# Turning softmax weights between attention and its values: 32x32 blocks on VectorE and DMA in the place of 128x128 turns on TensorE

## The chip, the cores and the metric

The kernel runs on one core of a Trainium2 chip, in one launch. The metric is device microseconds of that core, from runs without the profiler. A profiled execution of the kernel before gives the views below; times inside it are microseconds from the start of its span.

## The reference

Inputs are `x` (2 batches, 1024 tokens, 256 features), a context of 77 rows per batch, and the weights. Four residual layers follow one another, each on a layer normalization of `x` (no scale, no shift), all in 32-bit floats:

```python
x = x + cross_attention(ln(x), ctx, mask)            # 16 heads of 16, 77 keys
x = x + routed_attention(ln(x))                      # 4 of 16 heads of 64 per batch, 1024 keys
x = x + gelu(ln(x) @ ctx.T) @ ctx                    # 77 hidden units
x = x + moe(ln(x))                                   # 8 experts, one per token, 256 -> 1024 -> 256
```

The change lies in the second layer. Per batch, four heads are chosen by the mean over tokens of a router's logits. For each chosen head:

```python
score = softmax(Q @ K.T / 8)      # 1024 queries x 1024 keys
O = score @ V                     # then the 4 heads side by side, @ Wo + bo
```

The product with V sums over keys, and TensorE sums over partitions. The scores come out with queries on the partitions, so their exponentials have to be turned until keys lie on the partitions.

## The kernel before, in words

**Stages.** The kernel has three stages, with an order of instructions that is written out by hand for TensorE, VectorE, ScalarE and GpSimd (`tc.manual_schedule`). Stage "a" is cross attention, one step per tile of 128 tokens. Stage "b" is routed attention, with the third layer, the layer norms and the routing of the fourth worked in between. The tail and the expert blocks come last: 20 blocks of 128 token slots, each with its own expert weights of 2 MB.

**Items of stage b.** An item `i` is one tile of 128 queries with two heads (`m` names which two of the four); there are 32 (`NI`). Two tiles `q` = 0, 1 of the same two heads are a pair, `gm` (`TG` = 2). `split(i)` gives `gm, g, m, q`. Step `s` of stage b (`b_step`, L778) works on several items at once, in this order on each engine:

- `b_scores` (L693): for each of the two heads a PSUM tile `bsc` of 128 queries x 1024 keys, four matmuls in all. The pool `big` holds two such tiles, so the next item's scores need this item's exponentials to be done with them.
- `b_weights` (L712): VectorE finds the negative maximum of each row (L716); ScalarE takes the exponentials into `be` in SBUF and sums each row (L718).
- `b_transposed` (L722), called four times for the item of the step before: TensorE turns four 128x128 blocks of `be` into a PSUM tile `bpt` (L728), and ScalarE or VectorE copies it to `beT` (L729), two of the four each.
- `b_values` (L731), for the item three steps back (`VA`): half of the keys of a whole pair, 256 queries wide, into the PSUM tile `bov` that stays open for two steps (L738).
- `b_inverse_sums` (L744): VectorE inverts the sums, GpSimd spreads them over 64 columns; `b_turned_sums` (L752): TensorE turns these, ScalarE copies them to `brT`; `b_normalized` (L761): VectorE multiplies `bov` by `brT` into `boT` (L763), once per pair.
- `b_projected` (L765): from `boT` the output projection, added to `xs` (L774), five steps after the item's scores (`PR`).

**What fills the steps.** `at("b", s, pos, f, ...)` puts a piece of other work into step `s` at position 0, 2 or 3, and `take` runs it there: the projections of the routed heads (`b_qk` L646, `b_v` L665), the third layer (`do_rows "c"`, `do_turn "c"`, `c_hidden`, `gelu`, `c_out`), the routing of the fourth (`do_rows "d"`, `d_logits`, `d_expert`), and at the end of the stage the first expert list (`first_blocks`, `first_slots`, `first_tokens`, L1349 to L1367). `route_heads` (L570) of batch 1 runs in step 3 and has SP load that batch's chosen weights, 16 DMAs. Stage b's SBUF pool is `ebp` (L1470) with two buffers per tag.

**Queues.** DMAs of `ln_rows` (rows for the experts to DRAM, L305 and L306), of the routed weights (L612, L623) and of the expert weights (`block_loads`, L1083) are issued by SP, whose order the scheduler chose before. Rows of the expert blocks are gathered and scattered by GpSimd.

Of the kernel before, what the change touches and what calls it, by code (L numbers as in the profile page):

```python
# [20 lines left out]
P = 128  # L21
# [18 lines left out]
def kernel(  # L40
# [253 lines left out]
    def ln_rows(tag, t0, mv, rs, eng, y_out=None):  # L294

        ys = []
        for i in range(2):
            y = ynp.tile([P, D], F32, name=f"y_{tag}_{t0 + i}", tag="y")
            eng.tensor_scalar(
                y, xs[:, t0 + i, :], mv[:, i, 0:1], rs[:, i : i + 1], ALU.subtract, ALU.mult  # L300
            )
            ys.append(y)
            if y_out is not None:
                r0 = (t0 + i) * P
                nc.sync.dma_start(y_out[r0 : r0 + P, :D], y)  # L305
                nc.sync.dma_start(y_out[r0 : r0 + P, D:], xs[:, t0 + i, :])  # L306
        return ys

# [219 lines left out]
    sel, qks, vs = {}, {}, {}  # L528
    NP = NA // 2
# [116 lines left out]
    def b_qk(b, k, m, n, pool=accp, ptag="acc"):  # L646

        w, bc, _ = sel[b]
        if (b, k, m) not in qks:
            qks[b, k, m] = qkp[b].tile([P, S], F32, name=f"{k}T_{b}_{m}", tag=f"{k}T{m}")  # L650
        ps = pool.tile([P, 512], F32, name=f"bps_{b}_{m}_{k}_{n}", tag=ptag)
        for c in range(C):
# [6 lines left out]
            )  # L659
        nc.scalar.activation(  # L660
            qks[b, k, m][:, n : n + 512], ps, AF.Identity, bias=bc[k][:, m : m + 1],
# [3 lines left out]
    def b_v(b, t, pool=trp, ptag="tr"):  # L665
# [12 lines left out]
        nc.vector.tensor_tensor(vs[b][:, t], ps, bv, ALU.add)  # L678

# [13 lines left out]
    def b_scores(i):  # L693
# [15 lines left out]
        bes[i] = ebp.tile([P, 2, S], F32, name=f"be_{i}", tag="be")  # L709
        return sc  # L710

    def b_weights(i, sc):  # L712
        gm, g, m, q = split(i)
        for h in range(2):
# [4 lines left out]
                bes[i][:, h], sc[h], AF.Exp, bias=nm, accum_out=sms[g][:, q, s : s + 1]  # L719
            )  # L720

    def b_transposed(i, h, k0, copy):  # L722
        gm, g, m, q = split(i)
        if q == 0 and h == 0 and k0 == 0:
            beTs[gm] = ebp.tile([P, 2, NT, TG * P], F32, name=f"beT_{gm}", tag="beT")
        pt = trp.tile([P, 4, P], F32, name=f"bpt_{i}_{h}_{k0}", tag="tr")
        for k in range(k0, k0 + 4):
            nc.tensor.transpose(pt[:, k - k0, :], bes[i][:, h, k * P : (k + 1) * P], ident)  # L728
        copy(beTs[gm][:, h, k0 : k0 + 4, q * P : (q + 1) * P], pt)  # L729

    def b_values(i):  # L731
        gm, g, m, q = split(i)
        if q == 0:
            ovs[gm] = accp.tile([P, TG * P], F32, name=f"bov_{gm}", tag="acc")
        per = NT // TG
        for k in range(q * per, (q + 1) * per):
            for h in range(2):
                nc.tensor.matmul(  # L738
                    ovs[gm][h * FD : (h + 1) * FD, :],
                    lhsT=vs[g * TG // NT][:, k, 2 * m + h, :], rhs=beTs[gm][:, h, k, :],  # L740
# [20 lines left out]
    def b_normalized(gm):  # L761
        oT = oTs[gm] = ap_.tile([P, TG * P], F32, name=f"boT_{gm}", tag="boT", bufs=4)
        nc.vector.tensor_tensor(oT, ovs.pop(gm), rTs.pop(gm), ALU.mult)  # L763
# [12 lines left out]
    VA, PR = TG + 1, 2 * TG + 1  # L776

    def b_step(s):  # L778
# [3 lines left out]
        sc = b_scores(i) if i < NI else None  # L782
        take("b", s, 0)
        if 0 <= k < NI and k % TG == TG - 1:
            b_turned_sums(k // TG)
        if 0 <= j < NI:
            b_transposed(j, 0, 0, nc.scalar.copy)
        if i < NI:
            b_weights(i, sc)
        if 0 <= j < NI:  # L790
            b_transposed(j, 0, 4, nc.vector.tensor_copy)
        take("b", s, 2)
        if 0 <= k < NI:
            b_values(k)
        if 0 <= j < NI:
            b_transposed(j, 1, 0, nc.vector.tensor_copy)
            b_transposed(j, 1, 4, nc.scalar.copy)
            del bes[j]
            if j % TG == TG - 1:
                b_inverse_sums(j // TG)  # L800
        if 0 <= k < NI and k % TG == TG - 1:
            b_normalized(k // TG)
# [8 lines left out]
    def c_hidden(t0):  # L811
        b = t0 // NT
        yT = yTs.pop(("c", t0))
        ps = accp.tile([KC, 2 * P], F32, name=f"gps_{t0}", tag="acc")
# [6 lines left out]
    def c_gelu(t0):  # L821
# [8 lines left out]
        nc.vector.scalar_tensor_tensor(g, g, 1.0, ps, ALU.add, ALU.mult)  # L830

# [391 lines left out]
    def do_y(tag, t0, eng=nc.vector):  # L1223
        rows[tag, t0] = ln_rows(tag, t0, *rows[tag, t0], eng, ztok if tag == "d" else None)

    def do_rows(tag, t0, bias=None):

        do_power(tag, t0)
        do_y(tag, t0, nc.gpsimd)
        if bias is not None:  # L1230
            add_bias(t0, 2, bias)

# [66 lines left out]
    for t in range(NT):  # L1299
        at(*(("a", 18, 3), ("a", 18, 3), ("b", 0, 3), ("b", 0, 3),  # L1300
             ("b", 1, 2), ("b", 1, 2), ("b", 2, 2), ("b", 2, 2))[t], b_v, 0, t, *(acc if t > 3 else tr))
    for s, pos, k, m, n, *pool in (
        (5, 2, "k", 0, 0), (5, 3, "k", 0, 512), (6, 2, "q", 0, 0), (6, 3, "k", 1, 0),
        (7, 2, "k", 1, 512), (8, 2, "q", 1, 0), (19, 0, "q", 0, 512, *tr), (21, 0, "q", 1, 512, *tr),
    ):
        at("b", s, pos, b_qk, 1, k, m, n, *pool)
    for t in range(NT):
        at("b", 8 + t, 0, b_v, 1, t)

    def gelu(t0):  # L1310
        every(c_gelu(t0))

    for g in range(T // TG):
        s, t0 = 4 * g, TG * g
        if s + 13 < NI:
            at("b", s + 8, 3, do_rows, "c", t0)
            at("b", s + 9, 3, do_turn, "c", t0, *acc)
            at("b", s + 10, 2, c_hidden, t0)
            at("b", s + 10, 3, gelu, t0)
            at("b", s + 11, 2, c_out, t0)  # L1320
            at("b", s + 11, 3, do_rows, "d", t0)
            at("b", s + 13, 0, do_turn, "d", t0)
# [4 lines left out]
    at("b", 28, 3, do_rows, "c", t0)  # L1327
    at("b", 29, 3, do_turn, "c", t0, *acc)
    at("b", 30, 2, c_hidden, t0)
    at("b", 30, 3, gelu, t0)  # L1330
# [212 lines left out]
```

## Time and profile before

| what | us |
|---|---|
| median of 3 runs (622.35 to 623.37) | 623.32 |
| the profiled execution's own time | 623.49 |
| its span | 621.8 |
| TensorE busy, of the span | 581.7 |
| VectorE busy | 359.9 |
| ScalarE busy | 234.7 |
| GpSimd busy | 162.0 |

In the profile, PE is TensorE's matmuls, PEld its weight loads, which overlap them, DVE is VectorE, ACT ScalarE, POOL GpSimd, SP the engine that only issues DMAs. A line such as `L728 PE MATMUL bpt<-ident,be` names the line of the kernel, the engine, the operation, and the tile that is written and those that are read; then follow the shape, how often it occurs (`x512`), busy time in all, mean nanoseconds of one, and how long the engine was idle just before these instructions and which instruction ended most of that wait. A matmul of 32-bit floats shows as two instructions; a turn as one. In a view of stretches each row begins with the stretch and its length, then has the busy time of each engine in it, the granted TensorE clock as a share, the share of the DMA engines' time that was used, and GB/s.

Stage a ends and stage b begins near 152; the last scores of stage b start at 404.75; the steady run of expert blocks begins near 489 and lasts to the end.

### The profile page before, as it was taken

To read this page: it belongs to the slowest core of one execution; us is meant where nothing else is said; L and a number is where in the kernel's file an instruction comes from. 1 tells how busy PE (TensorE), PEld (TensorE's weight loads), DVE (VectorE), ACT (ScalarE), POOL (GpSimd) and SP (SyncE) were. 2 spreads that over 40 slices of the span, in tenths; PEclk is the share of its full clock that TensorE was granted. 3 is DMA by queue.
4 is the path that set the end of the run, shared out by engine and by line. 5 is a ranking of instruction groups with operands and counts; after the bars stand their busy time and mean duration, and the time that the engine had idled before them with its cause. 6 is when DMAs were issued, how large, how long until landed. Compare 5 with 4: busy or idle time off the path is not lost. (4 is left out here: it accounts for less than half of the span.)

```text
span 621.8 us, 10102 instructions
## 1 busy us (share of the span) xinstructions
PE 581.7 (94%) x3722; PEld 429.3 (69%) x3722; DVE 359.9 (58%) x939; ACT 234.7 (38%) x476; POOL 162.0 (26%) x204
## 2 busy tenths in 40 slices
PE   5999999989999999999999999996797999999994
PEld 4578878866655556656555656564596999999994
DVE  6767667852874356658665767676546433333331
ACT  3555545542655355445445555440021012111110
POOL 6656233222200020403021222200401233333321
PEclk9999999999999999999999999997689899999998
DMA  7100000020001000001000100011993799999940
GB/s 233 34 2 2 1 0 2 1 61 1 1 19 41 1 1 18 17 1 36 1 34 1 35 2 34 2 35 72 353 338 119 255 362 323 360 372 371 344 144 11
DMA packets 49674, 62.75 MB, mean 101 GB/s; under 512 B 11513, under 2 KB 42708, under 8 KB 49622
## 3 DMA queue, kind: packets, MB, share of 16 engines
q1 hardware_dynamic: 46352, 54.04, 25.8%
q0 software_dynamic: 2560, 7.34, 3.2%
q8 instruction: 31, 0.51, 0.3%
q10 hardware_dynamic: 709, 0.68, 0.3%
q14 instruction: 22, 0.17, 0.1%
HBM read 55.76 MB, written 6.82 MB: 101 GB/s over the span
## 5 line engine op out<-in xcount | busy, mean ns | idle before, releaser
L716 DVE TENSOR_REDUCE bnm<-bsc 128x1 f32<-128x1024 f32 x64 | 75.2, 1216 | 14.9 <-PE bsc L702 14.9
L1131 PE MATMUL ph<-ybT,w1s 128*128 128x128 f32 x640 | 79.7, 284 | 3.9 <-DVE ybT L1116 3.9
L1131 PEld LDWEIGHTS ph<-ybT,w1s 128*128 128x128 f32 x640 | 78.4, 200 | 6.0 <-DVE ybT L1116 5.1
L728 PE MATMUL bpt<-ident,be 128*128 128x128 f32 x512 | 73.1, 280 | 3.2 <-DVE v L678 1.2
L1150 PE MATMUL epo<-w2s,ehT 128*128 128x256 f32 x320 | 75.6, 380 | 0.0
L728 PEld LDWEIGHTS bpt<-ident,be 128*128 128x128 f32 x512 | 55.6, 140 | 27.9 <-issue 10.1
L718 ACT ACTIVATE be<-bsc,bnm 128x1024 f32<-128x1024 f32 x64 | 70.8, 1113 | 8.3 <-DVE bnm L716 7.9
L729 DVE COPY beT<-bpt 128x512 f32<-128x512 f32 x64 | 43.9, 686 | 50.4 <-PE bpt L728 50.4
L1138 ACT ACTIVATE ehT<-ph,b1s 128x128 f32<-128x128 f32 x80 | 22.9, 369 | 116.3 <-PE ph L1131 115.1
L702 PE MATMUL bsc<-kT,qT 64*128 64x512 f32 x256 | 64.6, 615 | 0.0
L738 PE MATMUL bov<-beT,v 128*64 128x256 f32 x512 | 63.4, 391 | 0.0
L1150 PEld LDWEIGHTS epo<-w2s,ehT 128*128 128x128 f32 x320 | 57.9, 190 | 6.3
L729 ACT COPY beT<-bpt 128x512 f32<-128x512 f32 x64 | 37.5, 586 | 62.4 <-PE bpt L728 61.4
L1140 DVE TENSOR_SCALAR ehT<-ph,b1s 128x128 f32<-128x128 f32 x80 | 22.5, 343 | 61.2 <-ACT ehT L1138 56.8
L738 PEld LDWEIGHTS bov<-beT,v 128*64 128x64 f32 x512 | 34.4, 139 | 24.6 <-issue 9.4
L1162 POOL DMA_INDIRECT out_dram<-ob,etok x20 | 20.5, 1023 | 94.2 <-DMA out_dram<-ob,etok 40.5
L750 POOL COPY brb<-brc 128x256 f32<-128x256 f32 x16 | 6.4, 398 | 146.5 <-DVE brc L748 146.5
L702 PEld LDWEIGHTS bsc<-kT,qT 64*128 64x128 f32 x256 | 22.5, 186 | 25.1 <-issue 20.7
L477 PE MATMUL av<-vblk,eT 128*128 128x51 f32 x320 | 37.4, 272 | 0.8 <-DVE hn L485 0.8
L477 PEld LDWEIGHTS av<-vblk,eT 128*128 128x128 f32 x320 | 37.1, 192 | 1.6 <-DVE hn L485 1.1
L453 DVE TENSOR_REDUCE mx<-sc 128x8 f32<-128x616 f32 x32 | 25.3, 792 | 16.6 <-PE sc L439 16.6
L469 ACT COPY eT<-pt 128x512 f32<-128x512 f32 (+1 forms) x48 | 23.0, 515 | 25.9 <-PE pt L468 25.1
(253 smaller groups left out, 854.2 us busy)
## 6 DMA issues: line engine op xcount, KB each, us to landing
w1s<-in_L_ffn_w_dram SPq DMA_DIRECT2D x20, 1024.0 KB
w2s<-in_L_ffn_w_dram SPq DMA_DIRECT2D x20, 1024.0 KB
b2s<-in_L_ffn_b_dram SPq DMA_DIRECT2D x20, 128.0 KB
xs<-in_x_dram SPq DMA_DIRECT2D x4, 512.0 KB
ztok<-xs SPq DMA_DIRECT2D x16, 128.0 KB
ztok<-y_d SPq DMA_DIRECT2D x16, 128.0 KB
ws_k<-in_L_ffn_Wk_dram SPq DMA_DIRECT2D x8, 64.0 KB
ws_q<-in_L_ffn_Wq_dram SPq DMA_DIRECT2D x8, 64.0 KB
```

Of the source, the lines that this page charges most:

```text
L453: nc.vector.tensor_reduce(mx, scv, AX.X, ALU.max)
L469: copy(eTs[t][:, c0 : c0 + n, :], pt[:, :n, :])
L477: nc.tensor.matmul(av[:, h0 : h0 + HW, :].rearrange("p h d -> p (h d)"), lhsT=eT[:, c, :], rhs=vblk[:, t // NT, c].rearrange("p h d -> p ( ...
L702: nc.tensor.matmul(sc[h][:, n : n + 512], lhsT=qks[b, "q", m][r, q0 : q0 + P], rhs=qks[b, "k", m][r, n : n + 512], start=True, stop=True,)
L716: nc.vector.tensor_reduce(nm, sc[h], AX.X, ALU.max, negate=True)
L718: nc.scalar.activation(bes[i][:, h], sc[h], AF.Exp, bias=nm, accum_out=sms[g][:, q, s : s + 1])
L728: nc.tensor.transpose(pt[:, k - k0, :], bes[i][:, h, k * P : (k + 1) * P], ident)
L729: copy(beTs[gm][:, h, k0 : k0 + 4, q * P : (q + 1) * P], pt)
L738: nc.tensor.matmul(ovs[gm][h * FD : (h + 1) * FD, :], lhsT=vs[g * TG // NT][:, k, 2 * m + h, :], rhs=beTs[gm][:, h, k, :], start=(k == 0), ...
L1131: nc.tensor.matmul(ph[:, f, :], lhsT=ws[n][0][:, c, f * P : (f + 1) * P], rhs=ybT[:, c, :], start=(c == 0), stop=(c == C - 1),)
L1138: nc.scalar.activation(hT[:, f, :], ph[:, f, :], AF.Relu, bias=b1s[:, f : f + 1])
L1150: nc.tensor.matmul(po, lhsT=hT[:, f, :], rhs=w2s[:, f, :], start=(f == 0), stop=(f == FC - 1))
```

## The change

The turn of `be` is done in two halves. VectorE turns `be` in place, in blocks of 32x32 (`b_turned`); that leaves each block turned but on its old quarter of the partitions. SP then issues 16 DMAs per pair (`b_moved`), each of 32 partitions x 4 KB, from quarter `g` of `be` to quarter `k` of `beT`. To make each of these one contiguous run per partition, the keys are stored in another order (the k-half of `b_qk`, and the reshaped `be`). TensorE turns none of it.

Along with that:

- `be` is one tile per pair and not per item; the values of an item are summed in one step over all 1024 keys and 128 queries, read in runs of 32 columns, and normalized per item;
- `VA` goes from 3 to 4 and `PR` from 5 to 4; the stage has one step less;
- the turns of an item stand at the start of the next step, ahead of that step's reduces on VectorE; the reciprocal of the sums stands ahead of the second item's turns;
- SP's order is now that of the program text, too; storing the rows for the experts is its own function at its own place (`store_rows`);
- many pieces of other work move by a step or a position, those of the end of the stage a step earlier, and `gelu` is spread over three positions.

```diff
+    def store_rows(t0, y_out):
+
+        for i, y in enumerate(rows["d", t0]):
+            r0 = (t0 + i) * P
+            nc.sync.dma_start(y_out[r0 : r0 + P, :D], y)
+            nc.sync.dma_start(y_out[r0 : r0 + P, D:], xs[:, t0 + i, :])
...
+    QD, QL = 4, 32
...
+        if k == "k":
+            out = qks[b, k, m].rearrange("p (g t l) -> p t g l", g=QD, l=QL)[:, n // P : n // P + 4]
+            ps = ps.rearrange("p (t g l) -> p t g l", g=QD, l=QL)
         nc.scalar.activation(
-            qks[b, k, m][:, n : n + 512], ps, AF.Identity, bias=bc[k][:, m : m + 1],
+            out, ps, AF.Identity, bias=bc[k][:, m : m + 1],
...
-        bes[i] = ebp.tile([P, 2, S], F32, name=f"be_{i}", tag="be")
+        if q == 0:
+            bes[gm] = ebp.tile([P, QD, TG, 2, S // QD], F32, name=f"be_{gm}", tag="be")
...
-                bes[i][:, h], sc[h], AF.Exp, bias=nm, accum_out=sms[g][:, q, s : s + 1]
-            )
-
-    def b_transposed(i, h, k0, copy):
+                bes[gm][:, :, q, h, :], sc[h].rearrange("p (g x) -> p g x", g=QD), AF.Exp, bias=nm,
+                accum_out=sms[g][:, q, s : s + 1],
+            )
+
+    def b_turned(i):
+
         gm, g, m, q = split(i)
-        if q == 0 and h == 0 and k0 == 0:
-            beTs[gm] = ebp.tile([P, 2, NT, TG * P], F32, name=f"beT_{gm}", tag="beT")
-        pt = trp.tile([P, 4, P], F32, name=f"bpt_{i}_{h}_{k0}", tag="tr")
-        for k in range(k0, k0 + 4):
-            nc.tensor.transpose(pt[:, k - k0, :], bes[i][:, h, k * P : (k + 1) * P], ident)
-        copy(beTs[gm][:, h, k0 : k0 + 4, q * P : (q + 1) * P], pt)
+        for h in range(2):
+            e = bes[gm][:, :, q, h, :]
+            nc.vector.transpose(e, e)
+
+    def b_moved(gm):
+
+
+        e = bes.pop(gm)
+        eT = beTs[gm] = ebp.tile([P, QD, TG, 2, NT, QL], F32, name=f"beT_{gm}", tag="beT")
+        for k in range(QD):
+            for g in range(QD):
+                nc.sync.dma_start(
+                    eT[k * QL : (k + 1) * QL, g].rearrange("l q h t x -> l (q h t x)"),
+                    e[g * QL : (g + 1) * QL, k].rearrange("l q h x -> l (q h x)"),
+                )
 
     def b_values(i):
         gm, g, m, q = split(i)
-        if q == 0:
-            ovs[gm] = accp.tile([P, TG * P], F32, name=f"bov_{gm}", tag="acc")
-        per = NT // TG
-        for k in range(q * per, (q + 1) * per):
+        ov = ovs[i] = accp.tile([P, P], F32, name=f"bov_{i}", tag="acc")
+        eT = beTs[gm]
+        for k in range(NT):
             for h in range(2):
                 nc.tensor.matmul(
-                    ovs[gm][h * FD : (h + 1) * FD, :],
-                    lhsT=vs[g * TG // NT][:, k, 2 * m + h, :], rhs=beTs[gm][:, h, k, :],
+                    ov[h * FD : (h + 1) * FD, :].rearrange("p (g x) -> p g x", g=QD),
+                    lhsT=vs[g * TG // NT][:, k, 2 * m + h, :], rhs=eT[:, :, q, h, k, :],
                     start=(k == 0), stop=(k == NT - 1),
                 )
...
-    VA, PR = TG + 1, 2 * TG + 1
+    VA, PR = 4, 4
...
         sc = b_scores(i) if i < NI else None
+        if 0 <= j < NI:
+            if j % TG == TG - 1:
+                b_inverse_sums(j // TG)
+            b_turned(j)
+            if j % TG == TG - 1:
+                b_moved(j // TG)
         take("b", s, 0)
-        if 0 <= k < NI and k % TG == TG - 1:
-            b_turned_sums(k // TG)
-        if 0 <= j < NI:
-            b_transposed(j, 0, 0, nc.scalar.copy)
         if i < NI:
             b_weights(i, sc)
-        if 0 <= j < NI:
-            b_transposed(j, 0, 4, nc.vector.tensor_copy)
-        take("b", s, 2)
         if 0 <= k < NI:
             b_values(k)
-        if 0 <= j < NI:
-            b_transposed(j, 1, 0, nc.vector.tensor_copy)
-            b_transposed(j, 1, 4, nc.scalar.copy)
-            del bes[j]
-            if j % TG == TG - 1:
-                b_inverse_sums(j // TG)
-        if 0 <= k < NI and k % TG == TG - 1:
-            b_normalized(k // TG)
+            b_normalized(k)
+        if 0 <= j < NI and j % TG == TG - 1:
+            b_turned_sums(j // TG)
+        take("b", s, 2)
...
-    at("b", 31, 2, do_power, "d", t0)
-    at("b", 31, 3, do_y, "d", t0)
-    at("b", 32, 2, do_turn, "d", t0, *acc)
-    at("b", 32, 3, d_logits, t0)
+    at("b", 30, 3, do_power, "d", t0)
+    at("b", 31, 2, do_y, "d", t0)
+    at("b", 32, 0, do_turn, "d", t0)
+    at("b", 32, 2, d_logits, t0)
...
-    at("b", 32, 3, do_power, "c", t0)
+    at("b", 31, 3, do_power, "c", t0)
...
-    at("b", 33, 3, first_blocks)
-    at("b", 33, 3, do_turn, "c", T1, *acc)
-    at("b", 34, 0, first_slots)
-    at("b", 35, 0, first_tokens)
+    at("b", 32, 3, first_blocks)
+    at("b", 32, 3, do_turn, "c", T1)
+    at("b", 33, 2, first_slots)
...
-            mybir.EngineType.Pool,
+            mybir.EngineType.Pool, mybir.EngineType.SP,
...
-            if s == NI + VA:
+            if s == NI + VA - 1:
                 stage_b.close()
+                pools["h"] = ctx.enter_context(tc.tile_pool(name="hp", bufs=2, side="right"))
                 pools["w", 1] = ctx.enter_context(tc.tile_pool(name="w1p", bufs=2, side="right"))
+                first_tokens()
```

## The prediction

> **What bounds the kernel now.** I read the page's engine shares and costliest groups first, then the busy times of the stretch in which routed attention runs (first scores to end of step 31), then the same for a cycle of four steps, then the order of instructions in two steps and at the end of the stage. From the page:
>
> ```profile
> PE 581.7 (94%) x3722; PEld 429.3 (69%) x3722; DVE 359.9 (58%) x939; ACT 234.7 (38%) x476; POOL 162.0 (26%) x204
> ...
> L716 DVE TENSOR_REDUCE bnm<-bsc 128x1 f32<-128x1024 f32 x64 | 75.2, 1216 | 14.9 <-PE bsc L702 14.9
> ...
> L728 PE MATMUL bpt<-ident,be 128*128 128x128 f32 x512 | 73.1, 280 | 3.2 <-DVE v L678 1.2
> ...
> L729 DVE COPY beT<-bpt 128x512 f32<-128x512 f32 x64 | 43.9, 686 | 50.4 <-PE bpt L728 50.4
> ```
>
> TensorE is busy nearly always, and 73.1 us of that are the turns that the change removes. Both copying engines wait for it at L729, not it for them. In the stretch (first row) and in four steps in the middle of it (the others), columns PE, PEld, DVE, ACT, POOL, clock, DMA:
>
> ```profile
> 152.40:412.70 260.30, 253.66 (x1553) 154.49 (x1552) 170.64 (x357) 131.27 (x241) 45.46 (x52) 1.00 0.05 15
> ...
> 335.34:342.51 7.17, 7.14 (x48) 4.19 (x47) 4.66 (x13) 3.84 (x7) 0.00 (x0) 1.00 0.00 0
> 342.51:350.08 7.57, 7.57 (x49) 4.75 (x49) 5.74 (x10) 4.75 (x9) 0.40 (x1) 1.00 0.10 35
> 350.08:357.25 7.17, 7.14 (x47) 4.31 (x46) 5.64 (x12) 3.77 (x7) 3.43 (x4) 1.00 0.12 39
> 357.25:366.46 9.21, 8.37 (x61) 5.69 (x61) 6.58 (x17) 3.96 (x7) 3.73 (x4) 1.00 0.00 1
> ```
>
> The 32 steps take 8.1 us each and TensorE fills them (253.7 of 260.3). VectorE stands at 66%, the DMA engines at 5%. The instructions of one step, which give the prices:
>
> ```profile
> 274.82 1.99 PE L702 MATMUL bsc<-kT,qT 64*128 64x512 f32 x8
> ...
> 278.25 2.34 DVE L716 TENSOR_REDUCE bnm<-bsc 128x1 f32<-128x1024 f32 x2
> ...
> 279.84 1.95 PE L738 MATMUL bov<-beT,v 128*64 128x256 f32 x16
> ...
> 280.66 1.11 ACT L718 ACTIVATE be<-bsc,bnm 128x1024 f32<-128x1024 f32 x1
> ...
> 281.72 1.09 PE L728 MATMUL bpt<-ident,be 128*128 128x128 f32 x8
> 281.81 0.80 SPq L306 DMA_DIRECT2D ztok<-xs  x2
> ```
>
> After the stage TensorE runs the expert blocks back to back (113.7 of the last 121.8 us), so an earlier end of the stage passes to the end of the kernel one for one.
>
> [...] No turn on VectorE is in this trace[...]. [...] This trace has only transfers over all partitions. [...]
>
> **The change, part by part,** all against the profiled execution (span 621.8, time 623.49; the median is 623.32, so no correction is due).
>
> *TensorE.* The 512 turns go: 73.1 us, 2.28 per item, of which 70.7 in the stretch (the bpt instructions there: 70.75). The values (L738) become twice as many instructions of half the columns, per item 32 of 128 instead of 16 of 256. The two heads' matmuls start together and 16 take 1.95 us, a pair each 0.24. At half the columns a pair should take half; the turns' 8 in 1.09 show that a load and a 128-column matmul can follow every 0.136. So 16 pairs take 1.95 to 2.2; I take 1.95, no change, and keep 0.25 x 32 = 8 us for the range. A gain is excluded, since the same columns stream. Rows in runs of 32 I take as free. TensorE's work falls to 253.7 - 70.7 = 183 us, 5.7 per step.
>
> *VectorE.* It loses its half of the copies: 41.8 us in the stretch (61 x 0.686). It gains 64 in-place turns, 62 of them in the stretch, of 1024 elements[...]. I take 1.24: 76.9 us. The normalizing (L763, 0.395 for 256 columns) becomes two of 128, at most 0.13 more per pair: 2 us. Sum 170.6 - 41.8 + 76.9 + 2 = 207.7 us, 6.5 per step. In the four steps above VectorE comes to 4.66+1.24 = 5.9, 7.0, 6.9 and 7.8, TensorE to 7.14-2.28 = 4.9, 5.3, 4.9 and 6.1. VectorE is what is late next in nearly every step.
>
> *ScalarE.* Loses 64 copies (37.5 us); the exponentials and the k-half of the projections write in strides at the same counts. It stays near 3 us per step: no cost, hidden beside VectorE.
>
> *Waits in the loop.* Scores of the next item need the PSUM of this one: 1.99 + 2.34 + 1.11 + 0.20 (reading the sum) = 5.65 us at least per step, below 6.5, but it leaves VectorE idle in the light steps, whose turns have only one short normalize in front of them. The turns stand ahead of the reduces on VectorE, so ScalarE's next exponentials wait behind them; they run while TensorE makes the scores. The reciprocal ahead of every second item's turns waits for both exponentials. GpSimd now gets the rows for "c" and "d" at one step (2.4 + 2.4 + 2 x 0.7 us) ahead of the copy of sums that TensorE turns. For all this 0.6 us per step, 19 us (bounds 0.2 and 1.0).
>
> *DMA.* Each pair of items moves 2 MiB within SBUF by 16 DMAs of 128 KB on SP. Issue: 0.40 each, 6.4 us. [...] I take 13. The values come two steps after the move is issued, and the same time covers the reuse of "be" by the exponentials: 2 x 7.1 = 14.2 us. Hidden, with one microsecond to spare; without the cover each microsecond costs 14 pairs x 1 us.
> SP is now in hand-written order. The loads of batch 1's routed weights (SP issues from 180 to 191.7 in the trace of before, 16 DMAs) stand between the moves of pairs 0 and 1. The second move starts some 10 us late, and the values of item 2 are due near 195: 7 us of stall, once. The stores of rows for the experts (4 DMAs per four steps, 1.6 us) fall in the steps between moves.
>
> *Stage sum.* 207.7 + 19 + 7 = 234 against 260.3: -26 us.
>
> *End of the stage.* Before, the last scores start at 404.75, the logits of tiles 10 and 11 at 419.24, the first expert list's matmul at 435.18. The change moves this chain a step earlier, and without turns and with the statistics of tiles 12 and 13 out of the chain (some 2.4 us at 423.6 to 425.8) its VectorE part should end about 6 us sooner after the last scores. The last move (13 us) is covered by that chain (420.8 to 434). -6 us, bounds -9 and 0.
>
> Total: 621.8 - 26 - 6 = 590 of span, + 1.7 around it = **592**.
>
> **The rivals.**
> *The moves become the bound (slower).* Place: the wait of the values for 16 DMAs. [...] Against it: the DMA engines are idle (5%), and the expert weights at the end flow at 372 GB/s. It decides from a move of 16.3 us, two of today's steps. [...] 14 x (19 - 16.3) = +38, -6 at the end: 655.
> [...] 2.3 us each: VectorE 207.7 + 62 x 1.07 = 274 us plus 5 of waits, against 260; -6: 636. [...]
> *Part is given back.* Moves of about 16 us or waits over 1 us per step hold the steps near 7.8: 32 x 0.3 = 10 gained, the end's gain halved: 610 to 623.
> That the change does not do what it says is out: in the built program no bpt instruction is left, and 64 turns and 256 moves are there.
>
> **How the numbers follow.** VectorE-bound as worked out: 0.57, own range 570 to 610 (waits 0.2 to 1.0: -13/+13[...]; end -3/+6; values +8). Part given back 0.12 (0.03 of it within 0.2%, about what a measurement of this kernel can tell from no change). Moves 0.18, slow turn 0.13. Faster 0.66, same 0.03, slower 0.31. The range takes in the slow turn and the near half of the moves' case: 570 to 645.
>
> **What would show it.** Turns near 1.24 us, in groups of two; steps near 7 us; VectorE over 85% busy in the stage and TensorE near 75%; values 1.95 per item; TensorE waiting for DMA ahead of the values once, at item 2, and nowhere else; logits of tiles 10 and 11 some 10 us after the start of the last scores. I am wrong if the values wait for DMA at every second step, if the turns take 2 us, or if gaps of TensorE let its granted clock fall below 1.00 within the stage, as it does at 410 to 450 (0.80).

## The result and the profile after

Changed: 648.72 us median of 4 runs (647.87 to 649.51), before 622.84 of 4 beside them: ratio 1.040, 95% interval 1.039 to 1.042. It is slower by 26 us where 31 us were to be won. From here on "the stage" is the stretch from the first scores to the end of step 31, which is put at 8.0 us after the start of that step's scores in every kernel; "the end" is what follows the start of the last scores, so the two overlap by 8 us. In the profiled executions:

| | before | after | forecast |
|---|---|---|---|
| stage | 260.3 | 276.65 | 234 |
| last scores to the end | 217.0 | 224.8 | 211 |

The page of the changed kernel: the engines' shares, the granted clock in 40 slices, the costliest groups.

```profile
PE 552.4 (86%) x3722; PEld 411.5 (64%) x3722; DVE 394.8 (61%) x955; ACT 198.8 (31%) x412; POOL 161.3 (25%) x204
...
PEclk9999999999988999778888898977699599999998
...
L712 PE MATMUL bsc<-kT,qT 64*128 64x512 f32 x256 | 86.3, 746 | 3.6 <-ACT be L730 3.5
...
L760 PE MATMUL bov<-beT,v 128*64 128x128 f32 x1024 | 69.9, 295 | 9.2 <-DMA beT<-be 8.2
L740 DVE STREAM_TRANSPOSE be<-be 128x1024 f32<-128x1024 f32 x64 | 75.3, 1215 | 0.2 <-DMA beT<-be 0.2
```

The turns have the price that was forecast (1215 ns) and the values wait for the moves almost nowhere. But the scores, which the change doesn't touch, take 746 ns each where L702 took 615 before (64.6 us in all there, 86.3 now), and the clock is below 9 tenths in slices of the stage. The stage and two of its steps, by the columns PE, PEld, DVE, ACT, POOL, clock, DMA, GB/s:

```profile
152.58:429.23 276.65, 223.08 (x1493) 131.97 (x1492) 205.13 (x373) 95.61 (x179) 45.46 (x53) 0.89 0.57 128
...
291.31:300.44 9.13, 4.25 (x43) 2.62 (x43) 8.81 (x18) 2.30 (x4) 6.60 (x7) 1.00 0.25 55
300.44:309.37 8.93, 8.93 (x66) 5.68 (x65) 4.66 (x10) 3.65 (x7) 0.00 (x0) 0.81 0.82 178
```

VectorE has 205.1 us of work (forecast 207.7), and 71.5 us besides in which it waits (forecast 26). The first of the two steps is VectorE's and leaves TensorE idle for half of it; in the next TensorE is full, at a clock of 0.81. Neither engine is the bound throughout. A clock of 0.89 over 276.65 us is 61 us at half speed; the trace's clock record has them as twelve pieces of 3.41 or 6.83 us ("halved pieces" below). Where one begins is seen in TensorE's own instructions (in brackets the idle time before one and what ended it):

```profile
348.24 0.44 PE L779 MATMUL brt<-ident,brb 128*128 128x128 f32 x2
348.51 0.60 PE L795 MATMUL po_b<-fwo_s,boT 128*128 128x256 f32 x2
351.36 0.82 PE L795 MATMUL po_b<-fwo_s,boT 128*128 128x256 f32 x2 [2.25 <-DVE boT L788]
352.11 3.65 PE L712 MATMUL bsc<-kT,qT 64*128 64x512 f32 x8
```

After 2.25 us without work the clock is halved from 351.81 to 355.22, and the scores in it take 3.65 us instead of 1.99. From 200 us to the end of the stage TensorE has eleven idle times of 2.2 us or more, and a halved piece begins 2.1 to 5.4 us after the start of each. The length of an idle time alone does not decide it, though: one more piece begins after an idle time of 1.67 us (at 277.66), and none after one of 1.66 us (at 227.14). In the kernel before TensorE is never idle for 1 us there, and its clock stays at 1.00. What ScalarE and TensorE waited for, and when the values waited (first the sums of waits over the whole execution, with times and the longest, then the one instruction):

```profile
ACT be L730 <- DVE bnm L728: 93.8, 26, 7.8
...
PE brt L779 <- POOL brb L772: 24.3, 6, 5.1
...
PE po_b L795 <- DVE boT L788: 14.9, 8, 2.8
```

```profile
208.20 3.68 PE L760 MATMUL bov<-beT,v 128*64 128x128 f32 x32 [7.76 <-DMA beT<-be]
```

The theory after this: TensorE's turns had filled the time in which the loop of scores, reduces and exponentials keeps TensorE waiting; without them its clock is halved and the loop slows down ("clock theory"). The rivals: VectorE's queue with turns and statistics ahead of the reduces, GpSimd's copy, the moves.

### The profile page after: what moved, and what is told of

It is laid out like the page before. It is cut to its first block, busy times and chain, and to the rows that moved or that the text cites. A ratio compares the mean times of both kernels' runs of the same rounds, so it can differ in the third digit from the quotient of the medians.

```text
span 646.1 us, 10452 instructions
## 1 busy us (share of the span) xinstructions
PE 552.4 (86%) x3722; PEld 411.5 (64%) x3722; DVE 394.8 (61%) x955; ACT 198.8 (31%) x412; POOL 161.3 (25%) x204
## 5 line engine op out<-in xcount | busy, mean ns | idle before, releaser
L730 ACT ACTIVATE be<-bsc,bnm 128x1024 f32<-128x1024 f32 x64 | 71.2, 1115 | 110.8 <-DVE bnm L728 93.8
L712 PE MATMUL bsc<-kT,qT 64*128 64x512 f32 x256 | 86.3, 746 | 3.6 <-ACT be L730 3.5
L760 PEld LDWEIGHTS bov<-beT,v 128*64 128x64 f32 x1024 | 61.9, 149 | 31.7 <-issue 14.7
L1152 PE MATMUL ph<-ybT,w1s 128*128 128x128 f32 x640 | 77.4, 279 | 1.0 <-DVE ybT L1137 1.0
L1171 PE MATMUL epo<-w2s,ehT 128*128 128x256 f32 x320 | 78.1, 388 | 0.0
L760 PE MATMUL bov<-beT,v 128*64 128x128 f32 x1024 | 69.9, 295 | 9.2 <-DMA beT<-be 8.2
L740 DVE STREAM_TRANSPOSE be<-be 128x1024 f32<-128x1024 f32 x64 | 75.3, 1215 | 0.2 <-DMA beT<-be 0.2
L712 PEld LDWEIGHTS bsc<-kT,qT 64*128 64x128 f32 x256 | 30.1, 223 | 43.3 <-issue 31.2
L1161 DVE TENSOR_SCALAR ehT<-ph,b1s 128x128 f32<-128x128 f32 x80 | 22.5, 344 | 45.5 <-ACT ehT L1159 41.6
L291 POOL TENSOR_TENSOR rs_d<-rs_d,minus_half 128x2 f32<-128x2 f32 x8 | 5.7, 712 | 126.7 <-DVE rs_d L290 126.7
L795 PE MATMUL po_b<-fwo_s,boT 128*128 128x256 f32 x64 | 18.8, 398 | 14.9 <-DVE boT L788 14.9
L779 PE MATMUL brt<-ident,brb 128*128 128x128 f32 x32 | 7.8, 328 | 24.4 <-POOL brb L772 24.3
```

The costliest lines, as they stand in the source:

```text
L712: nc.tensor.matmul(sc[h][:, n : n + 512], lhsT=qks[b, "q", m][r, q0 : q0 + P], rhs=qks[b, "k", m][r, n : n + 512], start=True, stop=True,)
L730: nc.scalar.activation(bes[gm][:, :, q, h, :], sc[h].rearrange("p (g x) -> p g x", g=QD), AF.Exp, bias=nm, accum_out=sms[g][:, q, s : s + 1],)
L740: nc.vector.transpose(e, e)
L760: nc.tensor.matmul(ov[h * FD : (h + 1) * FD, :].rearrange("p (g x) -> p g x", g=QD), lhsT=vs[g * TG // NT][:, k, 2 * m + h, :], rhs=eT[:, ...
L1152: nc.tensor.matmul(ph[:, f, :], lhsT=ws[n][0][:, c, f * P : (f + 1) * P], rhs=ybT[:, c, :], start=(c == 0), stop=(c == C - 1),)
L1161: nc.vector.tensor_scalar(hT[:, f, :], ph[:, f, :], b1s[:, f : f + 1], 0.0, ALU.add, ALU.max)
```

## The experiments

Stage times are each kernel's one profiled execution, which lies up to 3.3 us from the median of its runs; ratios are of medians, to the kernel before.

**x1: the turns' load put back as idle matmuls.**

```diff
+        for _ in range(16):
+            nc.tensor.matmul(ov, lhsT=ident, rhs=ident, start=True, stop=True)
         for k in range(NT):          # b_values, every item
```

> The changed kernel with 16 idle matmuls of 128 columns (identity by identity, overwritten afterwards) ahead of every item's values: 2.2 us of TensorE work per step put back, about what the turns took there. Clock theory (gaps of TensorE halve its clock, and the scores, which are on the loop, then take 3.8 us instead of 2.0): the granted clock in the routed stage goes back to 0.97 or more, the scores to 2.0 us each, and the stage from 276.7 to 255-265 us in spite of the added work; whole kernel 630 to 640. VectorE theory (the stage is set by VectorE's work and the order of its queue alone): nothing is gained, 649 us or up to 20 more where the idle matmuls come in the way.

697.1 us (ratio 1.118), stage 314.3 at a clock of 0.99. My sizing was wrong: a matmul of 128 columns costs 0.24 us, not a turn's 0.136, so 3.84 us per step went in, 123 us in all, and TensorE became the bound (300.7 of 314.3). It says only that 75 of 123 us did not lengthen the kernel (648.7 to 697.1), as they filled gaps and raised the clock (0.89 to 0.99).

**x2: no moves; x3: no turns on VectorE.**

```diff
-        e = bes.pop(gm) ... 16 DMAs                        # x2, b_moved
+        beTs[gm] = bes.pop(gm).rearrange("p g q h (t x) -> p g q h t x", t=NT)
-            nc.vector.transpose(e, e)                      # x3, b_turned
+            pass
```

Without moves `be` is held until the values have read it, so x2 (and x11, x12) has four buffers for it instead of two.

> The changed kernel with the moves left out: the values read the turned blocks where they lie, so the output is not the reference's, and the tokens' routing and the experts' blocks at the end may differ; the routed stage is what is compared (first scores to end of step 31, 276.7 us in the changed kernel). Clock theory: only the one stall ahead of item 2 goes (7.8 us), and the clock drops stay: 265 to 270 us. Moves theory (the transfers, their issue or their waits set the step): 255 us or less, with steps near 7.5 us.

> The changed kernel with the 32x32 turns on VectorE left out (the moves stay; the output is not the reference's; the routed stage is what is compared, 276.7 us in the changed kernel). VectorE theory: 2.4 us go from each step, stage 200 to 210 us. Clock theory: the loop of scores, reduces and exponentials stays, and TensorE has more gaps, not fewer, so that its clock falls further; 225 to 245 us, with scores of 3.7 us or more in over half of the steps. If the moves were the bound: over 265.

Their stages, x2 first:

```profile
152.53:415.43 262.90, 218.13 (x1494) 129.19 (x1493) 204.38 (x374) 95.78 (x179) 45.34 (x53) 0.91 0.05 14
```

```profile
152.57:405.83 253.26, 210.28 (x1522) 128.41 (x1523) 137.25 (x319) 97.42 (x181) 45.47 (x53) 0.93 0.63 141
```

x2: of the 13.75 us won, 9.5 are step 6 (18.21 to 8.67), where item 2's values wait for a move behind the weight loads, and 4.2 are steps 10, 14 and 15; from step 16 on each step is the same within 0.1 us. The moves don't set the step. x3: 23 us less, though VectorE's work falls by 67.9 us (and step 6 is 5 us longer): VectorE's work isn't the bound throughout either. Both keep a low clock (0.91, 0.93). Neither result lies in a range that was named beforehand.

**x4: the kernel before without its turns; x12: the changed kernel with neither turns nor moves.** These are the two floors, on which each way of turning stands. (x4 has a third buffer for `beT`, which the exponentials now fill.)

```diff
-                bes[i][:, h], sc[h], AF.Exp, ...           # x4: no b_transposed at all
+                beTs[gm][:, h, :, q * P : (q + 1) * P], sc[h].rearrange(...), AF.Exp, ...
```

> The kernel before with TensorE's turns and their copies left out, nothing in their place (exponentials go straight to where the values read; the output is not the reference's; routed stage compared, 260.3 us before). It asks what there is to win at all by taking the turns from TensorE. If TensorE's work alone set the stage (as before): 260.3 - 70.7 = 190 us at a granted clock of 1.00. Clock theory: the loop of scores, reduces and exponentials (5.65 us at least) opens gaps, the clock falls to 0.8 to 0.9, and the stage takes 205 to 230 us.

> The changed kernel with neither turns nor moves; the output is not the reference's and the routed stage is compared. Against the kernel before without its turns (216.5 us) it shows what the rest of the changed schedule costs; against the run without moves (262.9) what the turns on VectorE cost. If the schedule is free: 215 to 222 us, and the turns cost 40 or more. If the schedule (two rows at one step on GpSimd ahead of the inverse sums, fewer matmuls to cover it) costs much: 235 to 245 us, and the turns only 20 to 28.

Their stages, x4 first:

```profile
152.98:369.43 216.45, 207.06 (x1059) 107.52 (x1058) 133.40 (x297) 97.55 (x180) 45.75 (x53) 0.99 0.06 18
```

```profile
152.93:392.08 239.15, 210.37 (x1523) 128.82 (x1524) 137.16 (x319) 97.86 (x181) 45.60 (x53) 0.94 0.06 17
```

(Their whole times, 617.6 and 645.4, don't compare: without the turns the tokens are routed into 23 expert blocks instead of 20.) Without its turns the kernel before would lose 43.85 us of the stage, not the 70.7 that TensorE spends on them. Little of the other 26.9 us comes back as idle time of TensorE (9.4 us against 6.6). 13.4 of them were no time of the turns' own: in the kernel before other matmuls run beside the turns, and without the turns' instructions its TensorE is busy for 196.3 of the 253.7 us. The scores take the rest, 75.1 us instead of 64.6, since the eight matmul instructions of a step start further apart (2.35 us for them on the mean instead of 2.02, at 361.43 2.69), while each takes 621 ns against 615.

x4 also bears on the clock theory: its clock is 0.99, where 0.8 to 0.9 was expected. Taking the turns out of the old order leaves it there, so their absence alone is not what opens the gaps; in the changed order, with neither turns nor moves, it falls to 0.94. And that order costs 22.7 us with nothing in it. Steps 12, 16, 20, 24 and 28 are 4.2 to 5.0 us longer in x12 than in x4, 22.8 us together, and what the other steps win and lose cancels. Into these steps the changed order puts the statistics and rows of both the third and the fourth layer, and in them TensorE turns the inverse sums in the very step in which VectorE makes them, where the kernel before turns them two steps later. In step 16 of x12, GpSimd's copy of the sums comes behind four rows, 8.31 us after the scores' start, and TensorE's turn of them at 8.77; in x4 that turn comes at 1.92. Steps 16, 24 and 28 of x12 take 9.4 to 9.7 us with TensorE 4.5 us busy, and the step after each takes 9.7 to 9.9 with TensorE full; the scores of the whole of x12 take 671 ns each, those of x4 621. No kernel was run with only these two things put back.

So the ladder is: floor 216.45, schedule +22.7, turns +23.75 (x2 against x12), moves +13.75: 276.65. In the other order, over x3, the turns stand at +23.4 and the moves at +14.1. TensorE's turns stood at +43.85 on the floor of the kernel before.

**x5: ScalarE spreads the sums; x6: idle matmuls in the gaps alone.**

```diff
-        nc.gpsimd.tensor_copy(rb, rc...)                   # x5, b_inverse_sums
+        nc.scalar.copy(rb, rc...)
+        for _ in range(14 if gm % 2 else 0):               # x6, b_turned_sums
+            nc.tensor.matmul(pt[:, 0, :], lhsT=ident, rhs=ident, start=True, stop=True)
+        for _ in range(0 if q else 8):                     # x6, b_projected
+            nc.tensor.matmul(po[:, :P], lhsT=ident, rhs=ident, start=True, stop=True)
```

> The changed kernel with one instruction moved: ScalarE instead of GpSimd spreads the inverse sums (brb), so that TensorE's turn of them doesn't wait for the rows that GpSimd makes for the feed-forward and the experts. GpSimd theory (this wait, 5 us of TensorE at every fourth step, opens the gaps after which the clock halves): the gaps of 4.9 us at brt go, the scores after them take 2.0 us instead of 3.7, the stage falls from 276.7 to 262-268 us, the kernel to 632-640. Queue theory (VectorE's turns and statistics stand ahead of the reduces, and the reduces bound the loop): nothing moves but the place of the wait; 270 us or more, 642 or more.

> The changed kernel with idle matmuls put only where TensorE has its gaps: 14 ahead of the turned sums at every fourth step (3.4 us) and 8 ahead of the projection of each first tile (1.9 us). Nothing waits less; only TensorE is kept busy. Clock theory: the granted clock in the stage goes to 0.97 or more, all scores to 2.0 us, and the stage from 276.7 to 255-266 us, the kernel to 628-639. Queue theory: the clock rises too, but the step is set by VectorE's queue: within 3 us of the changed kernel's 276.7, or longer where the idle matmuls come in the way.

x5: 642.6 (1.029), stage 273.3, which is the outcome named for the queue theory. The wait for GpSimd is gone, but TensorE then waits for the exponentials (`[3.72 <-ACT be L730]` ahead of the scores at 297.28, which take 4.74 us), where it had waited 4.88 us for the copy: another wait stands behind it. x6: 643.6 (1.033), stage 266.5, just outside what was named for the clock theory; the row for the stage, and that for its part from step 8 on:

```profile
153.20:419.73 266.53, 235.52 (x1801) 159.07 (x1800) 204.01 (x373) 95.71 (x178) 45.35 (x53) 0.97 0.59 132
228.36:419.73 191.37, 177.24 (x1487) 125.30 (x1486) 158.92 (x299) 70.84 (x133) 39.74 (x46) 1.00 0.65 146
```

From step 8 on the changed kernel takes 205.97 us at 0.88, x6 191.37 at 1.00: 14.6 us won by adding work. The scores alone make up 14.4 of it (63.4 us there, 49.0 in x6), since most go back to some 2.0 us. In step 24 of the changed kernel TensorE is idle for 5.09 us ahead of the turned sums, and the scores after them take 3.55 us; in x6:

```profile
361.50 3.39 PE L779 MATMUL brt<-ident 128*128 128x128 f32 x28
364.79 0.44 PE L781 MATMUL brt<-ident,brb 128*128 128x128 f32 x2
365.16 1.99 PE L712 MATMUL bsc<-kT,qT 64*128 64x512 f32 x8
```

That is the clock's own price, shown. Ahead of step 8 x6 is 4.5 us longer than the changed kernel (75.16 against 70.68): item 2 waits for its move whatever the clock (13.3 us here), so the idle matmuls win nothing there.

**x7, x8, x10, x11: reduces ahead of turns on VectorE.** x7 swaps the two, x8 adds x5's edit, x10 also puts the normalizing ahead of the turns, x11 is x10 without moves.

```diff
-        b_turned(j), b_moved(...); take(0); b_weights(i, sc); b_values(k); b_normalized(k)
+        take(0); b_weights(i, sc); b_values(k); b_normalized(k); b_turned(j), b_moved(...)   # x10
```

> The changed kernel with the order on VectorE turned about in each step: the reduces of the new item ahead of the turns of the item before, the move still right after its turns. Queue theory: reduces start when the scores are there, the exponentials and the next scores come 1 to 2.5 us sooner per step; the stage falls from 276.7 to 235-250 us unless the later moves make the values wait (the price of that: 1 to 3 us at every second step, up to 40 us). Clock theory: the gaps at the turned sums and at the projection stay, so does the clock (0.87-0.92), and little is gained: 268 to 277 us.

> The edits of the two runs before together (ScalarE spreads the inverse sums; reduces ahead of turns). If both waits matter: stage 225 to 245 us, the kernel below 615. If the moves' wait takes their place: values waiting for DMA at every second step, stage 255 to 270.

> The changed kernel with VectorE's order in each step reduces, normalizing, turns and the move after them. In the run with reduces ahead of turns the normalizing stood behind the turns and held the projection on TensorE; here it doesn't. Queue theory in its second form (turns ahead of the reduces cost 1 us per step, and what took the gain there was the normalizing): stage 245 to 265 us against 276.7. Moves theory for this order (the moves are issued 2 to 4 us later in the step and the values wait for them at every second step): 275 to 290, with values waiting for DMA some 2 us each time.

> The changed kernel without moves (as in the run without moves, 262.9 us in the stage) and with VectorE's order reduces, normalizing, turns. It leaves the moves out, so the output is not the reference's; the routed stage is compared. If turns ahead of the reduces cost the loop time, and only the moves' latency made the other order slower: 235 to 250 us. If the order is no cause: 258 to 268 us.

Stages 288.6, 280.8, 294.5 and 255.9; kernels 657.0 (1.051), 651.1 (1.045), 671.2 (1.078) and 627.4 (1.005). (x11 leaves the moves out, so that its whole time doesn't compare.) Without moves the order is worth 7 us (262.9 to 255.9), between the two ranges named; with moves x8 and x10 come out longer than any range named. x10 loses 18 us: the move is issued later and two engines wait for it (waits of TensorE, then ScalarE, 220 to 420 us of x10):

```profile
PE bov L760 <- DMA beT<-be: 26.8, 7, 6.1
```

```profile
ACT be L730 <- DMA beT<-be: 39.8, 7, 8.1
```

The place of the turns ahead of the reduces is worth 7 us at most here, so it isn't the main cause. The moves have little slack: they are hidden only where the turns come first.

**x9: every second pair turned by TensorE again.** `b_transposed` in the new layout for odd `gm`, the exponentials of those pairs written so that each 128x128 block lies together.

> The changed kernel with the work shared out: the pairs of routed heads with odd number are turned by TensorE again (3 of 4 copies on ScalarE, 1 on VectorE), the even ones by VectorE and the moves. Per four steps VectorE has 2.4 x 2 us less of turns and 0.7 x 2 more of copies, TensorE 4.6 us more, and the moves are half as many, none of them at the stalled item 2 or at the end. If, as the runs so far say, gaps, clock and the one stall took the gain: the clock stays at 0.97 or more in the stage, step 6 falls from 18 to 9 us, four steps take 28 to 30 us, stage 235 to 255 us (276.7 in the changed kernel, 260.3 before), kernel 595 to 625. If the order of the queues sets the step whatever the load: 265 us or more.

641.3 (1.027), stage 266.1. The stall is gone (step 6 8.66 us) and the clock is 0.97, but four steps take 34 us. That is the outcome named for the order of the queues (265 or more), not for gaps, clock and stall alone. From 220 to 420 us ScalarE's copies of the turned blocks wait 41 us for TensorE, and TensorE 7.5 us for copies; that the turns fall into steps that are full already is my reading, which no run tests.

**x13, x14, x15: the causes out together.** x13 is x5 and x6 and batch 1's v weights loaded after the second move. x14 instead has TensorE turn the one stalled pair (`gm == 1`, as in x9) and no idle matmuls after the stage; x15 is x14 with GpSimd's copy kept.

> The changed kernel with the three causes found mended together: idle matmuls in TensorE's gaps (-6 us of the kernel by themselves), ScalarE spreads the inverse sums (-6), and batch 1's loads of v weights and bias issued after the second move instead of ahead of it (4.3 us of the 7.8 us stall). If they add: 649 - 6 - 6 - 4 = 633, and up to 8 us less where the early stall had eaten the gain of the clock: 624 to 634. If they overlap: 636 to 643.

> The changed kernel with idle matmuls in the gaps of the stage (none after it), ScalarE spreading the inverse sums, and the one stalled pair (items 2 and 3) turned by TensorE as before the change, so that its move does not stand behind the weight loads. Adding up: 259.9 us (stage of the run with all mended) less some 10 for the stall: 248 to 252 us in the stage; the end some 225 us from the last scores: kernel 622 to 630, about the kernel before. If another wait takes the stall's place: 256 us or more, 632 or more.

> The same with GpSimd spreading the inverse sums, as in the changed kernel. If the wait for GpSimd matters only through the gaps that it opens: within 2 us of the run beside it, since the idle matmuls fill the gaps. If it is on the loop by itself: 4 to 8 us slower.

x13: 637.8 (1.023); step 6 still took 20.1 us: the second move began at 193.9 instead of 195.3, since SP stood from 182 to 188 between two loads of k and q weights (182 to 185 in the changed kernel), so taking the v weights away moved it little. x14: 622.6 (0.998, interval 0.997 to 0.999), x15: 623.6 (1.000, 0.998 to 1.001). All 26 us of loss are gone. Once the gaps are filled, it makes no difference which engine spreads the sums: x14 and x15 are 1.1 us apart in the stage. The idle matmuls take 3.4 us at that place in both, so that GpSimd's wait mattered only through its gaps is likely, but not shown. The stage of x14, then that of x15 and its part from step 8 on:

```profile
152.60:403.05 250.45, 235.87 (x1805) 158.23 (x1804) 200.60 (x371) 104.27 (x199) 39.46 (x38) 0.99 0.59 133
```

```profile
152.37:403.90 251.53, 232.86 (x1805) 156.51 (x1804) 200.69 (x371) 98.92 (x184) 45.34 (x53) 1.00 0.58 132
212.30:403.90 191.60, 177.14 (x1487) 125.35 (x1486) 158.94 (x299) 70.86 (x133) 39.73 (x46) 1.00 0.65 146
```

The two mends add: in x15 the steps ahead of step 8 take 59.9 us instead of 70.7, where the stalled pair is turned by TensorE, and those from step 8 on 191.6 instead of 206.0, where the gaps are filled. But with its clock at 0.99 and without the stall, the stage of x14 is only 10 us shorter than before, not 26: VectorE still waits 50 us in it.

**x16, x17, x18: the end.** x16 is x15 with 32 idle matmuls ahead of the first expert block and 18 of 36 columns ahead of the second list; in x18 these 18 have 128 columns; x17 is the kernel before with 12 and 12 in its own gaps at the end.

> The run with the stall out and GpSimd spreading the sums, and idle matmuls in the two long gaps at the end too: 32 ahead of the first expert block (7.7 us), 18 ahead of the second list (4.1 us). Clock theory for the end: the 27 us of half clock there go, 6 to 11 us of time with them; from the last scores to the end 213 to 218 us instead of 223.8, the kernel 612 to 618, faster than both. If the chain is longer by itself: 222 us or more, 622 to 626.

> The kernel before, with idle matmuls in its gaps at the end (12 ahead of the first expert block, 12 ahead of the hidden layer of the fourth). It has 24 us of half clock there (427 to 485). If idle matmuls win without the change as well: 616 to 621 instead of 623. If its gaps are too short to matter: 622 to 625.

> As the run with the end filled, but the 18 idle matmuls ahead of the second list have 128 columns each instead of 36. If narrow matmuls count as idleness: no half clock between 470 and 500, from the last scores to the end 217 to 220 us instead of 223.8, the kernel 617 to 621. If the drop there comes from something else: it stays, 623 to 626.

x16: 624.3 (1.003), x17: 624.6 (1.003), x18: 619.1 (0.992, 0.990 to 0.994). The second list in x16, then in x18:

```profile
473.03 4.21 PE L1105 MATMUL tok<-ident 128*128 128x36 f32 x36 [0.89 <-DVE ob L1223]
477.07 6.77 PE L1110 MATMUL tok<-eblk,erow 128*128 128x36 f32 x32
```

```profile
472.12 4.18 PE L1107 MATMUL idle<-ident 128*128 128x128 f32 x36
477.05 3.76 PE L1109 MATMUL tok<-eblk,erow 128*128 128x36 f32 x32 [0.74 <-DVE eblk L1095]
```

The narrow idle matmuls did not hold the clock: the list's own matmuls take 6.77 us behind them; behind wide ones of the same duration they take 3.76. Slow matmuls stay in x18 where none were expected: from 480.64 ten of L1215 take 4.09 us (2.32 at 463.67), and from 495.79 the 32 of L1196 take 4.79 (3.73 at 485.65). The first filling had no gain to show: 13.65 us of half clock follow the first gap in the changed kernel, and with it filled the end of x16 stays at 223.8. With the second filled by wide ones it falls to 220.7 us, not to 217. x18 is the fastest kernel here that computes the reference's output. In the kernel before the idle matmuls bring nothing (x17), but there the clock hardly rose: 0.978 to 0.980 over its whole span, against 0.973 to 0.978 in the runs of the kernel before beside it.

## Why the prediction was wrong, point by point

- *TensorE.* The turns went, and the values kept their price (1.97 us for 32 against 1.95). Its busy time fell to 223.1 us, not to 183: the turns' 70.7 us were taken off whole, though 13.4 of them lay beside other matmuls, and much of the rest is half clock (x6 without its idle matmuls is at 198 us). And work taken from the busiest engine was not time won: x4 puts the most that could be won, in the order of the kernel before, at 43.85 us, 27 less than TensorE spent.
- *VectorE.* Right in its work: 205.1 us against 207.7, the turn 1.215 us against 1.24, an assumption that no trace of the kernel before showed. But that work fills 74% of the stage and not 85.
- *Waits in the loop*: the step that failed. I took 0.6 us per step, bounds 0.2 and 1.0; VectorE waited 71.5 us in the stage, 62 of them (1.9 per step) apart from the stall. Three things are in it. One is the clock, 14.6 us from step 8 on (x6). I had named it as what would make me wrong, and gave it neither a price nor a share of the range. In the changed kernel idle times of 2.24 us, and one of 1.67 us, were followed by half clock. The second is the changed order: rows of two layers in one step and the inverse sums turned at once cost 22.7 us with neither turns nor moves (x12 against x4; what its halved clock takes is in it, so the two don't add). I had listed the rows among the waits without a price of their own. The third is that the bound passes from engine to engine. I did compare the engines step by step, but in four steps of the kernel before, where VectorE is the later one in each (5.9, 7.0, 6.9, 7.8 us), and then took VectorE's sum for the stage. Steps 24 to 27 of x14, by the columns as above:

```profile
339.09:348.39 9.30, 7.43 (x71) 5.82 (x71) 8.98 (x19) 2.74 (x5) 6.24 (x6) 1.00 0.52 114
348.39:355.59 7.20, 7.20 (x66) 5.12 (x65) 4.99 (x10) 3.65 (x7) 0.00 (x0) 1.00 0.80 175
355.59:363.25 7.66, 6.91 (x64) 5.08 (x63) 6.93 (x18) 3.28 (x6) 0.00 (x0) 1.00 0.71 178
363.25:369.68 6.43, 6.30 (x49) 4.28 (x48) 5.91 (x7) 2.85 (x7) 0.00 (x0) 1.00 0.89 200
```

The larger of TensorE's and VectorE's time in each come to 29.4 of the 30.6 us, VectorE's alone to 26.8. (The idle matmuls in the first and third, 3.4 and 2.0 us, don't make TensorE the larger there.) This third part rests on the sums; no run tests it by itself.
- *DMA.* Right: the values waited once, 7.8 us (forecast 7), at item 2, behind batch 1's weight loads. From the first issue there (195.26) to the values' start (208.20) are 12.9 us, against 13; x10 gives 12.3. The 13 us were an assumption that no trace of the kernel before showed, and that the total agrees does not say what sets it: the issues took 10.1 us per move and more, not 6.4, and the packets of a move that runs alone (issued at 348.6) lie from 1.2 to 11.5 us after its first issue, 2.1 MB in 10.3 us, so that issuing may have set the pace. The moves' price in the stage was 13.75, some 4 beside the stall.
- *The end.* Forecast -6, measured +7.8. The logits of tiles 10 and 11 come 13.1 us after the last scores (14.5 before; I had said 10) and the first list 32.2 after (30.4 before): hardly a gain; halved pieces lie in these steps too, but no run shows that they hold it. The first expert matmul is at +45.5 against +44.5; the rest is lost behind it, where after the gaps of 9.1 and 4.8 us half clock lasts 27 us instead of 10, and the second list's matmuls take 7.04 us instead of 3.66. Filling the second gap wins 3 us back (x18), filling the first none (x16).
- *The rivals.* None came true as put. The slow turn of 2.3 us and the move of 19 us in two of them were assumptions of mine that no trace showed; the turn took 1.215 us, and the moves came to 12.3 to 12.9. "Part is given back" had the place (waits over 1 us per step), but not the size: at 1.9 per step more was given back than was won.

What stays open: how the schedule's 22.7 us divide between the wait for VectorE's statistics and GpSimd's rows and the clock, which at 0.94 over the 239.15 us of x12 makes up some 14 at most (an estimate from these two numbers); whether rows in separate steps and a later turn of the inverse sums would win them back; and the last 4 us of the end.

## What to carry to other kernels

Price what an engine's work fills before removing it: run the kernel with the operation simply left out and nothing in its place; that floor (here -44 us, not -71) is what a replacement can spend as long as the order around it stays. Then run the new order with nothing in it either: here it cost 23 us of the 44 before a turn or a move was made. Add the later of the engines step by step, in the new order and not over the stage, when the steps are tied by a loop. Look for gaps that are left to TensorE: in the changed kernel half clock of 3.41 or 6.83 us began 2.1 to 5.4 us after the start of each of eleven idle times of 2.2 us or more. Where the wait can't be removed, idle matmuls in the gap can keep the clock (from step 8 on 1.00 in x6 against 0.88; where a step had no gap they cost some 1.5 us, as in steps 6 and 8 of x14).

## What the runs showed of the hardware

- In the stage of the changed kernel the granted clock was at half for twelve pieces of 3.41 or 6.83 us, at the end for up to 13.65 us at a time. In the 3.41 us just before each of the twelve TensorE was busy for 0.48 of the time or less (1.65 us ahead of 280.12, nothing ahead of 205.03). The length of one idle time told less: half clock followed one of 1.67 us (at 277.66), and neither one of 1.66 us (at 227.14) nor, in x6, one of 1.80 us up to 359.61 (clock 1.00 from 355.82 to 365.16). In the kernel before, one piece (from 437.25) came after 3.41 us with TensorE busy for 2.81 us of them, most of that in matmuls of 10 columns.
- Matmuls of 36 columns that kept TensorE busy for 3.7 to 4.2 us were followed by slow matmuls in three kernels: in x4 (3.77 us of them from 437.51) the next eight of L1128 take 2.05 us and twelve of L1147 3.55, where twelve take 2.75 at 450.99; in x16 the list's take 6.77 us behind 4.21; in x18 ten of L1215 take 4.09 us behind 3.76. In the kernel before, 3.66 us of them from 485.77 were not (the clock is 1.00 from 485.04 to 618.16). With wide idle matmuls in the place of narrow ones the slow matmuls came later (x18). Why was not tried.
- A matmul of 128x128 in 32-bit floats takes 0.24 us in a row of them, a turn of the same size 0.136.
- Sixteen DMAs of 128 KB from 32 partitions to 32 others occupied SP for 10.0 to 11.3 us, 0.63 each or more, where its single loads took 0.37 to 0.39 (181.44 to 186.75 in the changed kernel); from first issue to use of the data, where the values waited for it, 12.3 to 12.9 us.
